# Layer 0 of a four-layer graph network: the degree sums in the text's order, the degrees ahead of a chunk's last products, and the second tile's rows ahead of the first pairs

## The chip, the core and the metric

The kernel runs on one core of one Trainium2 chip. The metric is the device time of one launch in microseconds, the median of several runs. The work is four layers in one program; the change touches the first of them alone.

## The reference, cut to what matters

`x` is 8 batches of 2048 nodes with 64 features, `adj` a 2048 x 2048 matrix, `H` a 2048 x 64 table of node to hyperedge. Layer 0 (the `h` that enters is a normalised, rectified `x`):

```python
def _L0_gnn_ref(x, H, adj, nhid, W, W_ind, a_node, a_gn, a_ge, fcW, fcb, av):
    h = x @ W
    s = leaky_relu(h @ a_node, 0.2)
    alpha = softmax(where(H.T[None] > 0, s[:, None, :], NEG), axis=-1)
    agg = einsum('ben,bnf->bef', alpha, h)
    beta = sigmoid((h @ a_gn)[:, None, :] + (agg @ a_ge)[:, :, None])
    all_he = elu(beta[..., None] * h[:, None] + (1 - beta[..., None]) * agg[:, :, None])
    deg = maximum(adj.sum(-1), 1.0)[:, None]
    industry = einsum('nm,bmf->bnf', adj / deg, x @ W_ind)
    ...                      # coefs1: softmax over the hyperedges of a node
    g = einsum('bne,benf->bnf', coefs1, all_he)
    pair = stack([industry, g], axis=2)
    ...                      # coefs2: softmax over the two, from tanh(pair @ fcW + fcb) @ av
    return einsum('bnk,bnkf->bnf', coefs2, pair)
```

Layers 1 to 3 follow: an attention over `adj`, three steps of message passing, and a polynomial graph convolution. They read the same `adj` and come after layer 0 in the data.

## The kernel before

Batches are taken two at a time, so a tile has 128 rows (2 x 64 features) and `NP` = 4 such pairs. Layer 0 goes through five stages, of which the change touches the second and the beginning of the third.

**First stage (to about 70 us).** The norm of `x` and the table `Y` = `x @ W_ind`, kept as two parts (`Y[0]`, `Y[1]`), together with the first quarter of the neighbour products.

**Second stage, the neighbour products (about 70 to 227 us).** `industry` is computed by column chunks of 512 nodes, `c` = 0 to 3. Chunk 0 belongs to the first stage. For chunks 1 to 3 the function `industry(c, own)` goes over 8 groups `g`. For each, `rows_of` requests a block `at` of 128 x 2 x 512 elements of `adjT` (512 KB) on GpSimd's DMA queue, into one of six buffers. A group has 16 products, 128x512 each, into four PSUM accumulators `acc`, one bank per batch pair, with no second buffer. A buffer `at` comes free when both the products and the degree sum of its group have read it. The degree of a node is the column sum of `adjT`: VectorE adds up the blocks in `ds` (L1066, 128x1024), and at the end of a chunk two products with a matrix of ones (L1078) sum over the partitions.

Between the products stand small pieces of other work, the `units`. Sixteen node tiles (`members`) each have two pieces `part` and one `end`. A `part` is: product `ph` (L1113), ScalarE copy `hi` (L1117), VectorE rest `lo` (L1118), the leaky relu `es` (L1121 to 1123) and VectorE product `hs` (L1124). The `end` is the product `pg` (L1136) and `pd` (L1140). `hi` and `lo` are stored to DRAM by SyncE, and have two buffers each. Other units build the lists of hyperedges (`ranks`, `numbers`, `widths`), the tables of hyperedge values (`table_1` to `table_5`) and the biases of the last layer (`biases`, which stores a tile `bs` of the tag `ev`).

At the end of a chunk `out_of` copies the accumulators into four tiles `ev` (tag `ev`, four buffers), takes the larger of degree and 1 (`rdeg`, L1080), and returns further units: the inverse by ScalarE's Ln and Exp (L1085, L1086), four products of `ev` and `rdeg` on VectorE (L1089), and four stores to `ind_dram` (L1090).

**Third stage, the pairs of node and hyperedge (about 227 to 360 us).** 18 tiles of 114 nodes, three groups of pairs each. `nodes(i)` makes the matrix `sT` that spreads a tile's nodes over its pairs: ScalarE's `tmp` (L823), then GpSimd's `sT` (L824); a tile `tmp` has one buffer. TensorE then makes `px`, VectorE `oT`, TensorE `pts` (against the identity `ident_r`) and `pm`, ScalarE the copy `S` and the sigmoid's tanh `be` (L1331). For each group of pairs TensorE makes `pd` and `pa`, VectorE `mix` and `ex`, ScalarE an exponential, GpSimd the weights, TensorE the sum `pgs`. These steps run in an order written out by hand.

**What sets the order.** The program is built by a layer that schedules instructions by their dependences and estimated readiness, engine by engine. An instruction that is issued through `InOrder` (the names `V`, `A`, `G`, `S` in layer 0) or passed to `keep_in_program_order` stays at its place in the text. Most units of the second stage, the degree sum and the evacuation among them, are issued through `nc.vector`, `nc.scalar` and the plain `mm`, and are placed by the scheduler.

The places in question, quoted short:

```python
if g > 0:
    nc.vector.tensor_tensor(ds, (was if g == 1 else ds).bitcast(FP), at.bitcast(FP), op=OP.add)
was = at
...
for step in (ranks, edges, turn, turned, shares, shared):
    step(0)
V, A = strict
next_nodes(1)
```

Of the kernel before, what the change touches and what calls it, by code (L numbers as in the profile page):

```python
# [16 lines left out]
P = 128  # L17
# [601 lines left out]
HN = N // 2  # L619
LN_EXP = "natural_log_exp_and_others"  # L620


# [148 lines left out]
def layer0(kit, hn, x1_dram, open_early, late_tile, between):  # L771
# [30 lines left out]
    etab = lst.tile([P, 2 * B], FR, name="etab")  # L802
    rden = lst.tile([P, LT, B], FP, name="rden")

    def of(i):
# [27 lines left out]
    with ExitStack() as sA:  # L833
# [107 lines left out]
        def rows_of(c, g):  # L941
            at = sp.tile([P, 2, CW], FR, tag="at", name="at")
            nc.gpsimd.dma_start(
                out=at,
                in_=t["adjT"][g * 2 * P : (g + 1) * 2 * P, cols(c)].bitcast(FR).rearrange("(k p) n -> p k n", p=P),
            )
            return at
# [91 lines left out]
        with ExitStack() as s1:  # L1039
# [7 lines left out]
            def industry(c, own):  # L1047

                for _ in range(2):
                    units.pop(0)()  # L1050
                acc, ds = accs(), dsp.tile([P, 2, CW], FR, tag="ds", name="ds")
                for g in range(NT // 2):
                    at = rows_of(c, g)
                    for k in range(2):
                        m = 2 * g + k
# [8 lines left out]

                    if g > 0:
                        nc.vector.tensor_tensor(ds, (was if g == 1 else ds).bitcast(FP), at.bitcast(FP), op=OP.add)  # L1066
                    was = at
                return out_of(c, acc, ds)

            def out_of(c, acc, ds):  # L1070
                ev = [sb.tile([P, CW], FP, tag="ev", name="ev", bufs=4) for p in range(NP)]
                for p in range(NP):
                    (nc.scalar.copy if p % 2 else nc.vector.tensor_copy)(ev[p], acc[p])
                deg = ds
                if c:
                    deg = ps.tile([P, CW], FP, tag="ph", name="deg", bufs=2)
                    for k in range(2):
                        mm(deg, ones_r, ds[:, k, :], start=k == 0, stop=k == 1)  # L1078
                rdeg = sb.tile([P, CW], FP, tag="rdeg", name="rdeg", bufs=1)
                nc.vector.tensor_scalar(rdeg, deg, 1.0, None, op0=OP.max)  # L1080
                nc.vector.tensor_reduce(bad[:, 3 + c : 4 + c], deg, AX.X, OP.min)
                nc.vector.tensor_scalar(bad[:, 3 + c : 4 + c], bad[:, 3 + c : 4 + c], 0.5, None, op0=OP.is_lt)

                def inverse():
                    nc.scalar.activation(rdeg, rdeg, AF.Ln, scale=2.0)  # L1085
                    nc.scalar.activation(rdeg, rdeg, AF.Exp, scale=-1.0)  # L1086

                def shares(p):
                    nc.vector.tensor_mul(ev[p], ev[p], rdeg)  # L1089
                    nc.sync.dma_start(out=ind_dram[p, :, cols(c)], in_=ev[p])  # L1090

                return [inverse] + [lambda p=p: shares(p) for p in range(NP)]

# [169 lines left out]
            units += [first_nodes, lambda: biases(3)]  # L1263
            own = out_of(0, acc, degs)
            for c in range(1, NCW):
# [9 lines left out]
    with ExitStack() as s0:  # L1275
# [8 lines left out]
        flat = lambda a: a.rearrange("p b f -> p (b f)")  # L1284
        ident_r = sb.tile([P, P], FR, name="ident_r", bufs=1)
        nc.vector.tensor_copy(ident_r, ident)
        def next_nodes(i):
# [100 lines left out]
        def done(i):  # L1388
            pt = tiles[i].pop("pb")
            for p in range(NP):  # L1390
                A.activation(gT[p][:, of(i)], pt[:, p, 0:LN], AF.Identity, bias=neg1)

        strict, V, A = (V, A), nc.vector, nc.scalar
        for step in (ranks, edges, turn, turned, shares, shared):
            step(0)
        V, A = strict
        next_nodes(1)

# [861 lines left out]
```

## Time and profile before

| | |
|---|---|
| median of 3 runs | 1966.83 us (1963.56 to 1970.12) |
| the profiled execution's own time | 1963.12 us |
| its span, first to last instruction | 1961.3 us |
| granted TensorE clock, mean | 0.989 |
| TensorE busy | 1900.6 us, 97% of the span |
| VectorE busy | 1190.7 us, 61% |
| ScalarE busy | 438.0 us, 22% |
| GpSimd busy | 315.4 us, 16% |

In the lines of the timeline each row has the start, the length, the engine, the line of the source, the operation, the tiles it writes and reads, the shape, the count, and in brackets the time for which the engine stood idle before it and what ended that. PE is TensorE, PEld its weight loads, DVE VectorE, ACT ScalarE, POOL GpSimd, SP SyncE; a q behind the name is the queue that issues. In rows by stage the clock is the share of the full TensorE clock that was granted. A matmul's listed length contains the part in which the next one already runs: of two 128x512 products in a row the second starts 0.23 us after the first.

### The profile page before, as it was taken

To read this page: it belongs to the slowest core of one execution; us is meant where nothing else is said; L and a number is where in the kernel's file an instruction comes from. 1 tells how busy PE (TensorE), PEld (TensorE's weight loads), DVE (VectorE), ACT (ScalarE), POOL (GpSimd) and SP (SyncE) were. 2 spreads that over 40 slices of the span, in tenths; PEclk is the share of its full clock that TensorE was granted. 3 is DMA by queue.
4 is the path that set the end of the run, shared out by engine and by line. 5 is a ranking of instruction groups with operands and counts; after the bars stand their busy time and mean duration, and the time that the engine had idled before them with its cause. 6 is when DMAs were issued, how large, how long until landed. Compare 5 with 4: busy or idle time off the path is not lost.

```text
span 1961.3 us, 23490 instructions
## 1 busy us (share of the span) xinstructions
PE 1900.6 (97%) x9060; PEld 1134.5 (58%) x9060; DVE 1190.7 (61%) x1917; ACT 438.0 (22%) x923; POOL 315.4 (16%) x435
## 2 busy tenths in 40 slices
PE   7999999889999999999999999999999999999997
PEld 6877777423323232257775477764577755677653
DVE  8676499768999998953326642346623275523365
ACT  6322355573111110111210111301112201112100
POOL 4111177310000000000002110012200022101122
PEclk9999899999999999999999999999999999999998
DMA  7556485473221212223101011100122011121000
GB/s 216 168 177 178 134 235 147 113 187 76 55 54 46 64 38 60 60 55 83 60 11 30 27 58 54 49 17 24 31 65 59 22 25 30 44 70 49 3 21 12
DMA packets 86362, 142.43 MB, mean 73 GB/s; under 512 B 33800, under 2 KB 34056, under 8 KB 83568
## 3 DMA queue, kind: packets, MB, share of 16 engines
q1 hardware_dynamic: 65200, 83.86, 14.3%
q0 software_dynamic: 21040, 56.98, 11.9%
q8 instruction: 73, 1.20, 0.3%
q14 instruction: 49, 0.40, 0.1%
HBM read 106.85 MB, written 37.09 MB: 73 GB/s over the span
## 4 chain that ended last, share of the span: by engine, by line
PE 66%; issue 17%; DVE 6%; DMA 4%; ACT 3%; POOL 3%; SPq 0%; POOLq 0%; DVEq 0%; ACTq 0%
PE acc L734 28%; PE u L734 14%; PE o L734 4%; PE py L734 3%; PE pd L734 2%; PE dn L734 2%; PE pgs L734 2%; PE acc L1058 2%; DMA at<-in_adjT 1%; PE var L734 1%; PE mean L734 1%; DMA den<-d_dram 1%; PE pv L734 1%; PE pf L734 1%; PE pm L734 1%
## 5 line engine op out<-in xcount | busy, mean ns | idle before, releaser
L734 PE MATMUL acc<-aT,parts 128*128 128x512 f32 x1664 | 448.2, 415 | 0.0
L734 PEld LDWEIGHTS acc<-aT,parts 128*128 128x128 f32 x1664 | 306.5, 188 | 102.2 <-issue 39.8
L2135 DVE TENSOR_TENSOR pr<-u,embf 128x512 f32<-128x512 f32 x256 | 170.7, 688 | 171.2 <-PE u L734 163.5
L734 PE MATMUL u<-W3f,y 64*128 64x512 f32 x1024 | 243.3, 589 | 0.0
L1733 DVE SCALAR_TENSOR_TENSOR pt<-R,wd,aT 128x1024 f32<-128x1024 f32 x192 | 236.2, 1280 | 9.5 <-DMA R<-r_dram 4.5
L734 PE MATMUL o<-pt,hS 128*64 128x512 f32 x1024 | 237.5, 599 | 0.8 <-DVE pt L1733 0.6
L734 PEld LDWEIGHTS u<-W3f,y 64*128 64x128 f32 x1024 | 101.8, 187 | 118.6 <-issue 118.6
L734 PEld LDWEIGHTS o<-pt,hS 128*64 128x64 f32 x1024 | 68.3, 136 | 160.2 <-issue 149.5
L734 PE MATMUL u<-W3f,v 64*128 64x512 f32 x512 | 137.9, 607 | 0.0
L2147 POOL TENSOR_TENSOR fold<-fold 128x256 f32<-128x256 f32 x64 | 47.7, 746 | 506.3 <-DVE fold L2146 506.3
L734 PE MATMUL dn<-pt,vd 128*32 128x512 f32 x1024 | 123.1, 598 | 0.0
L1952 DVE TENSOR_TENSOR yb<-py,cb_f 128x512 f32<-128x512 f32 x32 | 22.1, 691 | 161.4 <-PE py L734 161.4
L1058 PE MATMUL acc<-at,Y 128*128 128x512 f32 x384 | 105.1, 416 | 0.0
L734 PE MATMUL acc<-aTl,parts 128*128 128x512 f32 x384 | 96.5, 393 | 0.0
L2042 POOL TENSOR_TENSOR bq<-bq,xp 128x512 f32<-128x512 f32 x16 | 20.6, 1287 | 432.7 <-ACT xp L2025 432.7
L2139 DVE TENSOR_TENSOR pr<-pr 128x512 f32<-128x512 f32 x128 | 88.2, 689 | 2.2
L1733 DVE SCALAR_TENSOR_TENSOR pt<-R,wd,aTl 128x1024 f32<-128x1024 f32 x64 | 79.8, 1282 | 12.4 <-PE dn L734 8.2
L734 PEld LDWEIGHTS u<-W3f,v 64*128 64x128 f32 x512 | 51.4, 186 | 56.1 <-issue 34.1
L734 PEld LDWEIGHTS acc<-aTl,parts 128*128 128x128 f32 x384 | 72.1, 188 | 16.9
L1058 PEld LDWEIGHTS acc<-at,Y 128*128 128x128 f32 x384 | 70.6, 194 | 14.7 <-issue 1.3
L734 PEld LDWEIGHTS dn<-pt,vd 128*32 128x32 f32 x1024 | 26.9, 108 | 80.9 <-issue 77.1
L2113 ACT COPY y<-acc 128x512 f32<-128x512 f32 x16 | 9.4, 585 | 279.7 <-PE acc L734 279.7
(354 smaller groups left out, 2697.0 us busy)
## 6 DMA issues: line engine op xcount, KB each, us to landing
at<-in_adjT POOLq DMA_DIRECT2D x32, 512.0 KB, 5.5
raw<-in_adjT SPq DMA_DIRECT2D x64, 256.0 KB, 3.4
aT<-in_adjT POOLq DMA_DIRECT2D x12, 1024.0 KB, 5.5
xp<-xd SPq DMA_DIRECT2D x45, 256.0 KB, 3.0
R<-r_dram SPq DMA_DIRECT2D x14, 512.0 KB, 3.7
hlo<-lo_dram POOLq DMA_DIRECT2D x18, 235.1 KB, 3.9
hhi<-hi_dram POOLq DMA_DIRECT2D x18, 235.1 KB, 3.4
hi_dram<-hi SPq DMA_DIRECT2D x16, 264.0 KB, 3.4
```

The source lines that it names most:

```text
L734: one = self.nc.tensor.matmul(*args, **kw)
L1058: mm(acc[p], Y[h][:, m, p, :], at[:, k, :], start=m + h == 0, stop=m == NT - 1 and h == 1)
L1733: nc.vector.scalar_tensor_tensor(pt, R[b2], wd[:, m, b2 : b2 + 1], aT[m][:, s].bitcast(FP), op0=OP.max, op1=OP.mult)
L1952: nc.vector.tensor_tensor(yb, py, bias[:, None, :].to_broadcast([P, 4, P]), op=OP.add)
L2042: nc.gpsimd.tensor_add(bq, bq, xp)
L2113: nc.scalar.copy(y2, acc)
L2135: nc.vector.tensor_tensor(a, u[h], emb[:, i, 8 * w : 8 * w + 8, None].to_broadcast([P, 8, F]), op=OP.mult)
L2139: nc.vector.tensor_add(pr[h], pr[h], a)
L2147: nc.gpsimd.tensor_add(fold[:, :, 0:2, :], fold[:, :, 0:2, :], fold[:, :, 2:4, :])
```

## The change

The edits are these.

- The degree sum is issued through `V`, and ahead of its group's products instead of behind them.
- The two products for the degree are issued ahead of the last group's products and kept in the text's order; the maximum, Ln and Exp follow them there (`degrees`, `inverse`).
- In chunks 1 to 3 the accumulators of batch pairs 0 and 2 are multiplied by `rdeg` as VectorE reads them out of PSUM, and stored at once. Pairs 1 and 3 are copied by ScalarE as before and multiplied later, on GpSimd in chunk 3 and on VectorE otherwise. Chunk 0 keeps its copies and later products.
- The rounded identity `ident_r` is made at the start of layer 0, in a pool that lives to the end of the third stage.
- The table set that holds exp and tanh is loaded, and `next_nodes(1)` issued, ahead of tile 0's first steps in the third stage.

```diff
+TANH_EXP = "exp_and_others"
...
+    ident_r = lst.tile([P, P], FR, name="ident_r")
+    nc.vector.tensor_copy(ident_r, ident)
...
+                rdeg = None
                 for g in range(NT // 2):
                     at = rows_of(c, g)
+                    if g > 0:
+                        V.tensor_tensor(ds, (was if g == 1 else ds).bitcast(FP), at.bitcast(FP), op=OP.add)
+                    was = at
+                    if g == NT // 2 - 1:
+                        rdeg = degrees(c, ds)
                     for k in range(2):
...
-                    if g > 0:
-                        nc.vector.tensor_tensor(ds, (was if g == 1 else ds).bitcast(FP), at.bitcast(FP), op=OP.add)
-                    was = at
-                return out_of(c, acc, ds)
-
-            def out_of(c, acc, ds):
-                ev = [sb.tile([P, CW], FP, tag="ev", name="ev", bufs=4) for p in range(NP)]
-                for p in range(NP):
-                    (nc.scalar.copy if p % 2 else nc.vector.tensor_copy)(ev[p], acc[p])
-                deg = ds
-                if c:
-                    deg = ps.tile([P, CW], FP, tag="ph", name="deg", bufs=2)
-                    for k in range(2):
-                        mm(deg, ones_r, ds[:, k, :], start=k == 0, stop=k == 1)
+                return out_of(c, acc, rdeg)
+
+            def inverse(c, deg):
                 rdeg = sb.tile([P, CW], FP, tag="rdeg", name="rdeg", bufs=1)
                 nc.vector.tensor_scalar(rdeg, deg, 1.0, None, op0=OP.max)
+                nc.scalar.activation(rdeg, rdeg, AF.Ln, scale=2.0)
+                nc.scalar.activation(rdeg, rdeg, AF.Exp, scale=-1.0)
                 nc.vector.tensor_reduce(bad[:, 3 + c : 4 + c], deg, AX.X, OP.min)
                 nc.vector.tensor_scalar(bad[:, 3 + c : 4 + c], bad[:, 3 + c : 4 + c], 0.5, None, op0=OP.is_lt)
-
-                def inverse():
-                    nc.scalar.activation(rdeg, rdeg, AF.Ln, scale=2.0)
-                    nc.scalar.activation(rdeg, rdeg, AF.Exp, scale=-1.0)
+                return rdeg
+
+            def degrees(c, ds):
+                deg = ps.tile([P, CW], FP, tag="ph", name="deg", bufs=2)
+                for k in range(2):
+                    tc.keep_in_program_order(mm(deg, ones_r, ds[:, k, :], start=k == 0, stop=k == 1))
+                return inverse(c, deg)
+
+            def out_of(c, acc, rdeg):
+                ev = [sb.tile([P, CW], FP, tag="ev", name="ev", bufs=4) for p in range(NP)]
+                store = lambda p: nc.sync.dma_start(out=ind_dram[p, :, cols(c)], in_=ev[p])
+                late = {"rdeg": rdeg}
+                for p in range(NP):
+                    if p % 2:
+                        nc.scalar.copy(ev[p], acc[p])
+                    elif rdeg is None:
+                        nc.vector.tensor_copy(ev[p], acc[p])
+                    else:
+                        nc.vector.tensor_mul(ev[p], acc[p], rdeg)
+                        store(p)
 
                 def shares(p):
-                    nc.vector.tensor_mul(ev[p], ev[p], rdeg)
-                    nc.sync.dma_start(out=ind_dram[p, :, cols(c)], in_=ev[p])
-
-                return [inverse] + [lambda p=p: shares(p) for p in range(NP)]
+                    (nc.gpsimd if c == NCW - 1 else nc.vector).tensor_mul(ev[p], ev[p], late["rdeg"])
+                    store(p)
+
+                if rdeg is None:
+                    first = [lambda: late.update(rdeg=inverse(c, degs))]
+                    return first + [lambda p=p: shares(p) for p in range(NP)]
+                return [lambda p=p: shares(p) for p in (1, 3)]
...
-        ident_r = sb.tile([P, P], FR, name="ident_r", bufs=1)
-        nc.vector.tensor_copy(ident_r, ident)
...
+        tc.keep_in_program_order(nc.scalar.preload_act_table_set(TANH_EXP))
+        next_nodes(1)
         strict, V, A = (V, A), nc.vector, nc.scalar
         for step in (ranks, edges, turn, turned, shares, shared):
             step(0)
         V, A = strict
-        next_nodes(1)
```

More of the change, by code (lines that the diff above doesn't have):

```diff
@@ L1263, in layer0 @@
             units += [first_nodes, lambda: biases(3)]
-            own = out_of(0, acc, degs)
+            own = out_of(0, acc, None)
             for c in range(1, NCW):
```

## The prediction

> **What bounds the kernel now.** I read the page first, then busy time by stage, then the waits and the order of time inside layer 0, the only part that the change touches.
>
> ```profile
> span 1961.3 us, 23490 instructions
> PE 1900.6 (97%) x9060; PEld 1134.5 (58%) x9060; DVE 1190.7 (61%) x1917; ACT 438.0 (22%) x923; POOL 315.4 (16%) x435
> ```
>
> TensorE is occupied for 97% of the span, so a gain must come from its few idle microseconds or from stretches in which its clock is halved. By stage (columns: stretch, length, busy PE, PEld, DVE, ACT, POOL, granted clock, DMA):
>
> ```profile
> 69.00:117.00 48.00, 46.08 (x235) 36.19 (x234) 38.57 (x119) 12.50 (x46) 5.71 (x8) 1.00 0.65 196
> 117.00:172.00 55.00, 51.37 (x270) 40.81 (x269) 34.56 (x124) 13.60 (x48) 9.18 (x13) 1.00 0.63 185
> 172.00:227.00 55.00, 52.02 (x264) 41.25 (x263) 22.73 (x60) 13.73 (x32) 2.67 (x4) 0.94 0.31 94
> 227.00:246.00 19.00, 15.58 (x56) 12.81 (x55) 13.99 (x25) 9.37 (x19) 8.53 (x10) 0.65 0.99 304
> 246.00:360.00 114.00, 114.00 (x544) 81.01 (x543) 108.33 (x170) 62.78 (x164) 86.18 (x99) 1.00 0.58 165
> ```
>
> Chunks 1 to 3 of the neighbour products take the first three rows: TensorE idles 1.92 + 3.63 + 2.98 = 8.53 us. The fourth row is the start of the pairs: 3.42 us idle, and the clock at 0.65. From 246 on TensorE is full. The waits (who for whom: total, times, longest) say why it idles, the timeline shows the largest case:
>
> ```profile
> DVE ds L1066 <- DMA at<-in_adjT: 12.2, 8, 3.5
> PE ph L1113 <- DVE hs L1124: 7.6, 5, 2.9
> 126.63 0.71 POOL L943 DMA_DIRECT2D at<-in_adjT  x1 [7.40 <-PE acc L1058]
> 133.68 1.23 DVE L1066 TENSOR_TENSOR ds<-ds,at 128x1024 fp32r<-128x1024 f32 x1 [3.49 <-DMA at<-in_adjT]
> 134.82 0.42 DVE L1124 TENSOR_TENSOR hs<-ph,es 128x256 f32<-128x256 f32 x1
> 135.39 0.69 PE L1113 MATMUL ph<-W0x,hn 128*128 128x132 f32 x4 [2.92 <-DVE hs L1124]
> ```
>
> Counted by their loads, the degree sums run about five groups ahead of the products: this block is group 6 of chunk 2, whose products end near 172. VectorE stands 3.49 us before a block that has not landed, `hs` stands behind the sum, and TensorE waits 2.92 us for `hs`. At the start of the pairs:
>
> ```profile
> 228.94 0.52 PE L734 MATMUL pts<-ident_r,sT 114*128 114x114 f32 x3 [1.43 <-DVE bad L1082]
> 228.63 0.57 ACT L1073 COPY ev<-acc 128x512 f32<-128x512 f32 x1
> 230.09 1.28 ACT L1331 ACT_TABLE_LOAD   x1
> 231.55 0.61 ACT L823 ACTIVATE tmp<-slot,mid 114x384 f32<-114x384 f32 x1
> 232.26 1.23 POOL L824 TENSOR_SCALAR sT<-tmp,width 114x384 fp32r<-114x384 f32 x1 [43.00 <-ACT tmp L823]
> 233.55 0.69 PE L734 MATMUL px<-sT,Q 114*128 114x384 f32 x1 [1.99 <-POOL sT L824]
> 233.00:246.00 13.00, 12.45 (x37) 10.59 (x38) 8.76 (x14) 5.34 (x11) 7.80 (x10) 0.50 1.06 310
> ```
>
> The second tile's ranks wait for `sT`, that for `tmp`, that for the table load and the reciprocal before it. Then the pairs run 13 us at half clock.
>
> **What the Trainium skill says.** (1) "TensorE: Matmul & The Clock Gate", Part 1: the clock is full or half, granted by how busy a free-running window of 3.413 us was. The trace agrees: beside the row at 0.50, the clock is 0.57 in 181 to 185, after the 2.04 us gap that ends at 180.07. (2) The same page, "Architectural detail": ScalarE and VectorE take their queues strictly in order; the wait above shows it. (3) "ScalarE: Activation LUTs", "What ACT_TABLE_LOAD costs": 1283 ns for the load, and a drain for which I find no separate row; here it is 1.28 us and the next activation follows at 231.39.
>
> **The change, part by part.**
>
> *Sums in text order.* In the built order a chunk has 7 sums as before (21 x 1.22 us), now one before each group's products. A block is requested when the group six before it is done; 24 groups in 157 us are 6.6 us each and a landing takes about 5.5, so a block has landed some four groups (26 us) before its sum. VectorE no longer waits there. Of TensorE's six gaps (0.54, 1.38, 2.92, 0.70, 2.04, 0.95: together the 8.53) four lie behind such a sum: 1.38 + 2.92 + 2.04 + 0.95 = 7.29 us. The half-clock spell at 181 goes with its gap: 4 us x (1 - 0.57) = 1.7. Together **-9.0**. The sums move out of the full first chunk (11 run before 117, 7 do afterwards; VectorE is 38.6 of 48 us busy there) into the third, where it is busy 22.7 of 55. What is late next is the pipeline of members: the 2.27 us reduction of `MT` (L927), which began at 102.16, now stands before an `hs` and right behind the wait for a store (to 86.80). By the order of the queue that `hs` ends near 90.2 instead of 89.0; I charge **+1.0** (0 to 2).
>
> *Degrees ahead of the last products.* The two `deg` matmuls (0.46 us) stand four products before a chunk's end and can wait for sum 7. The last `hs` before that sum comes from a `ph` 3.7 us ahead of `deg`; `hi`, `lo`, `es`, `hs` and the sum take 3.4: about no wait. The banks `acc` are single, so the next chunk's first products now wait for the inverse: from the start of `deg`, 0.7 + maximum 0.7 + Ln 0.63 + `hi` 0.4 + Exp 0.63 + copy or product 0.69 = 3.8 us, while TensorE has 0.46 + 0.92 + ph 0.45 + pg 0.86 + ph 0.45 + pd 0.12 = 3.3 of other work: 0.5 at each of two turns, **+1.0** (0 to 4, as VectorE may be behind). Six PSUM copies (0.69) go from VectorE and two products of chunk 3 go to GpSimd (1.29 each by the nearest row, `bq` at L2042): off the path. The four stores stay, on SP; two move ahead of a member's stores, which nothing waits for within 5 us.
>
> *Identity early.* One cast (0.22 us) moves to the start, where VectorE idles 2.40 us before 7.92: nothing (0 to 0.2).
>
> *Start of the pairs.* Let T = 226.87 be the end of the products. `pts` no longer waits for the identity, but `pm` needs `oT`. `px` ends at T + 0.34, `oT` follows (0.55), `pm` takes 1.0, the first pair 0.9: TensorE stops at about T + 2.95. On ScalarE the queue is `ev` 3, table, `tmp`, `S`, `be`. In the built program `ev` 3 takes the buffer of the last bias store and must wait for its landing; before, that came at 227.92 and lay behind the reciprocal's Ln. Now the bias copy stands behind Ln and Exp, some 0.3 later: landing at T + 1.35. Then copy 0.57, table 1.28, `tmp` 0.61, `sT` 1.25 and 0.05 us between each: `px` of tile 1 at T + 5.2, against 233.55 = T + 6.7. GpSimd's two products end by T + 3.4, before `tmp` is there. So **-1.5**. The idle time is still about 2.2 us behind 1.0 us of 16-column products, so I keep the half-clock spell.
>
> Sum: -9.0 + 1.0 + 1.0 - 1.5 = **-8.5 us**. Nothing after the pairs is changed but the order of some loads on GpSimd, so it passes on whole. The sum is made against the profiled execution, which took 1963.12 us beside its span of 1961.3; the median of the runs is 1966.83, 3.7 above. On the median: 1966.8 - 8.5 = 1958.3, rounded to **1958**.
>
> **Rivals.**
> (a) *The clock stays full at the start of the pairs.* For: windows with gaps of 0.95 and 1.4 us (197, 228) did not halve it. Against: the idle of 2.2 us is as long as the 2.04 that did. Gain 13.65 / 2 = 6.8 more, four windows: 1951.5.
> (b) *The members' chain is the real bound.* Removing VectorE's wait only exposes the next one: `hi` and `lo` have two buffers, and VectorE also stood for their stores (to 86.80 and 96.73). For: VectorE is 80% busy in the first chunk. Against: it waited for blocks 12.2 us in all, and sums leave that chunk. Then 2 or 3 us are left of the gain: 1964.
> (c) *Slower: the turn of a chunk.* Products wait for the inverse, and that for sum 7 in a busy queue. It must eat the gain of 10.5 (9.0 + 1.5) and 5.9 more: 16.4 over three turns, 5.5 each, of which a half-clock window is 1.7; it decides from a wait of 3.8 us at every turn. The longest wait for VectorE's own work, without a block behind it, was 0.70. Then 1973.
> That the change doesn't do what it says is excluded by the built order for the sums.
>
> **How the numbers follow.** My case 58%, (a) 15%, (b) 20%, (c) 7%. Low end: (a) with both charges at zero, -17.3, gives 1949.5; high end: (b) with a scatter of 2 us, 1966. What a measurement of this kernel can tell from no change is 0.3%, 5.9 us. My case passes it nine times in ten, (a) always, (b) one time in four: faster 0.72, same 0.21, slower 0.07.
>
> **What would show it.** Right: in the waits, `ds <- DMA at` near zero; TensorE idle in the products under 4 us instead of 8.5; the pairs' first `px` of tile 1 about 5 us after the last product, behind a table load that waited for the bias store. Wrong: TensorE waiting for `ds` before `deg`, or for `ev` before a chunk's first products, by over 2 us; or `ph` waiting for `hs` as long as before.

## The result, and the profile after

The changed kernel took 1966.53 us (median of 12 runs, 1958.26 to 1972.23), the kernel before, beside it on the same chip, 1968.13 (12 runs, 1963.56 to 1973.2). The ratio of the two sets of runs is 0.9986, 95% interval 0.9970 to 1.0002 (the medians alone differ by 1.6 us): some 3 us were won, where 8.5 were forecast, and no change at all is not excluded. A later, longer comparison of the same two kernels (`r1_after`, 22 runs against 55) gives 0.9977, interval 0.9967 to 0.9987, or 4.5 us. The profiled execution of the changed kernel took 1963.18 us beside a span of 1961.3, as that of before did (1963.12 and 1961.3).

The page of the changed kernel, span and busy time of each engine:

```profile
span 1961.3 us, 23478 instructions
PE 1902.1 (97%) x9060; PEld 1132.4 (58%) x9060; DVE 1187.5 (61%) x1909; ACT 438.0 (22%) x923; POOL 318.6 (16%) x437
```

The same five stretches of layer 0 as in the prediction (stretch, length, busy PE, PEld, DVE, ACT, POOL, granted clock, DMA share, GB/s):

```profile
69.00:117.00 48.00, 46.16 (x234) 36.07 (x234) 34.75 (x115) 11.88 (x46) 5.71 (x8) 1.00 0.66 193
117.00:172.00 55.00, 52.45 (x265) 40.84 (x264) 33.32 (x119) 12.74 (x47) 9.33 (x13) 0.97 0.64 185
172.00:227.00 55.00, 53.77 (x285) 43.20 (x284) 29.09 (x68) 18.41 (x40) 5.75 (x7) 0.97 0.40 126
227.00:246.00 19.00, 17.35 (x64) 13.65 (x65) 14.23 (x23) 7.90 (x16) 12.67 (x15) 0.73 0.96 272
246.00:360.00 114.00, 112.77 (x533) 79.39 (x532) 109.10 (x172) 63.61 (x165) 84.81 (x97) 1.00 0.57 158
```

VectorE gave 4 us of work out of the first stretch and took 6 into the third, as said. TensorE is idle less in the second and third. But the clock of the second stretch, which was 1.00, is now 0.97, and 246 to 360, which was full, has 1.23 us of idle time: the pairs end 6 us earlier, so that the first gaps of their end lie inside it. The waits of the changed kernel (who for whom: total, times, longest; three lines of the list) show what came in place of `ds <- DMA at`, which is gone from the list:

```profile
DVE hi L1125 <- DMA hi_dram<-hi: 6.6, 4, 2.9
PE pf L735 <- DMA iv<-ind_dram: 5.3, 3, 2.6
PEld pm L735 <- DMA hlo<-lo_dram: 1.3, 1, 1.3
```

The first two were 1.9 and 2.7 us before; the third was not there. The timeline of TensorE, lines that waited:

```profile
86.97 0.69 PE L1132 MATMUL ph<-W0x,hn 128*128 128x132 f32 x4 [0.89 <-DVE es L1141]
111.88 0.72 PE L1132 MATMUL ph<-W0x,hn 128*128 128x132 f32 x4 [0.65 <-DVE rank L897]
116.75 0.70 PE L1088 MATMUL deg<-ds,ones_r 128*128 128x512 f32 x2 [0.30 <-DVE ds L632]
120.49 2.36 PE L1067 MATMUL acc<-at,Y 128*128 128x512 f32 x9 [0.24 <-ACT ev L1097]
158.37 0.72 PE L1132 MATMUL ph<-W0x,hn 128*128 128x132 f32 x4 [2.13 <-DVE rank L916]
...
227.78 0.69 PE L735 MATMUL px<-sT,Q 114*128 114x384 f32 x1 [1.63 <-POOL sT L827]
241.02 0.28 PE L735 MATMUL pm<-hlo,sT 114*128 114x16 f32 x1 [0.87 <-DMA hlo<-lo_dram]
```

With one more of 0.13 us (`deg` at 170.31) the gaps in the products come to 4.3 us, where they were 8.5. Of these, 3.7 us lie ahead of a `ph` and 0.7 at the two turns of a chunk, that is, between the last products of one chunk and the first of the next (`deg` and the first `acc`). The longest, 2.13 us ahead of `ph`, is put down to `rank`. VectorE's own timeline tells what `rank` stood behind:

```profile
156.31 0.07 DVE L1125 MEMSET hi<- 128x8 f32 x1 [2.66 <-DMA hi_dram<-hi]
157.77 0.54 DVE L916 TENSOR_TENSOR rank<-rank,pm 114x384 f32<-114x384 f32 x1 [1.40 <-issue]
157.79 0.07 DVE L1125 MEMSET lo<- 128x8 f32 x1
```

A memset of 65 ns waits 2.66 us for the store of an earlier member (issued 151.19, landed 5.06 us later), and everything else on VectorE stands behind it. For the 1.40 us ahead of `rank` the profile names no cause, but they end with the other memset: the store of `lo` landed at 157.73, and its memset starts 0.06 us later, just as that of `hi` starts 0.06 us after its own store (156.25). So VectorE stood about 4 us for two stores, TensorE waits for `rank`, and a half-clock spell of 3.4 us follows at 159.2. This is the wait on which the rest of this document turns.

**By stage.** Worked out from the traces. A chunk runs from its first product to the next chunk's first (the third: to its last product), "start" from the last product to the ranks of the sixth tile of pairs, "output" from the ranks of the last tile to layer 1's first attention product. In brackets: idle TensorE, and half of TensorE's occupied time at half clock, which is what the halved clock cost.

| us | before | before again | after | after again |
|---|---|---|---|---|
| chunk 1 | 50.0 (1.9, 0) | 50.3 (2.2, 0) | 51.0 (2.1, 0) | 50.4 (1.5, 0) |
| chunk 2 | 54.1 (3.6, 0) | 55.3 (3.1, 1.7) | 54.9 (2.3, 1.7) | 54.2 (3.2, 0) |
| chunk 3 | 52.4 (3.0, 3.4) | 55.7 (3.0, 6.8) | 47.4 (0, 1.7) | 53.8 (0, 8.5) |
| start | 37.0 (3.4, 6.3) | 35.8 (3.4, 4.8) | 34.8 (2.9, 5.0) | 35.9 (3.8, 5.1) |
| output | 105.3 (19.7, 4.3) | 105.9 (19.8, 4.8) | 110.2 (21.6, 7.3) | 107.4 (19.9, 6.2) |

Idle times of one kernel repeat within 1 us (1.7 in the output stage), the loss to the clock does not: chunk 3 of one and the same kernel lost 1.7 us in one execution and 8.5 in another.

### The profile page after: what moved, and what is told of

Same layout as the page of the kernel before. It is cut to its first block, busy times and chain, and to the rows that moved or that the text cites. A ratio compares the mean times of both kernels' runs of the same rounds, so it can differ in the third digit from the quotient of the medians.

```text
span 1961.3 us, 23478 instructions
## 1 busy us (share of the span) xinstructions
PE 1902.1 (97%) x9060; PEld 1132.4 (58%) x9060; DVE 1187.5 (61%) x1909; ACT 438.0 (22%) x923; POOL 318.6 (16%) x437
## 4 chain that ended last, share of the span: by engine, by line
PE 68%; issue 16%; DVE 5%; DMA 5%; ACT 4%; POOL 2%; SPq 0%; POOLq 0%; DVEq 0%; ACTq 0%
PE acc L735 28%; PE u L735 14%; PE acc L1067 4%; PE o L735 4%; PE py L735 3%; PE pgs L735 2%; PE dn L735 2%; PE pd L735 2%; PE var L735 1%; PE mean L735 1%; DMA den<-d_dram 1%; DMA iv<-ind_dram 1%; PE pv L735 1%; DMA W3f<-in_L_gnn_weight 1%; PE pm L735 1%
```

## The experiments

Each kernel goes by a label (`r1_sums`). All ratios are to the kernel before, run beside it on the same chip; its medians there were 1966.5 to 1971.2 us.

### Both kernels once more

> The kernel before, unchanged, for a second profile. Theory 1 (the waits belong to the kernel): TensorE idles 8 to 9 us in the neighbour products again, the last product starts at 226.5 +- 1, the last tile of pairs reaches its ranks at 351.4 +- 2, the output stage follows with a half-clock spell near 379 only. Theory 2 (the places are a matter of how the 3.4 us clock windows happen to fall): idle times of waits are as before, but the half-clock spells lie elsewhere, and milestones differ from the first profile by 3 us or more. Time by both: ratio 1.000 within 0.003.

Measured: 0.9990 (0.9976 to 1.0004), 14 runs; the last product started at 231.14 instead of 226.49, since chunks 2 and 3 had 17.1 us at half clock instead of 6.8 (5.1 us more lost to the clock).

> The changed kernel, unchanged, for a second profile. Theory 1: the last product starts near 222.7, the last tile of pairs near 345.1, 6 us ahead of before; then 3 us go in half-clock windows at the end of the pairs and 2.6 us in a wait for the fifth load of the industry term, so that the output stage ends only 1.3 us ahead, as in the first profile. Theory 2: the 6 us are there again, but one or both of the later losses are absent or lie elsewhere, because a window decides them. Time: ratio 0.9986 within 0.003.

Measured: 0.9977 (0.9967 to 0.9987). The table above has both. The waits of the products and of the start are there again, those of the output stage too; but the 6 us lead at the end of the pairs is 0.3 here against the first profile of before (4.1 against the second), eaten by half-clock spells at 203.6 and 213.9. Theory 2 holds for the clock, theory 1 for the waits. A single profile of this kernel can't be read to better than about 5 us unless idle time and clock are kept apart.

### The sums alone, and sums with the new start

```diff
                     at = rows_of(c, g)
+                    if g > 0:
+                        V.tensor_tensor(ds, (was if g == 1 else ds).bitcast(FP), at.bitcast(FP), op=OP.add)
+                    was = at
...
-                    if g > 0:
-                        nc.vector.tensor_tensor(ds, (was if g == 1 else ds).bitcast(FP), at.bitcast(FP), op=OP.add)
-                    was = at
```

> The kernel before with one part of the change: the degree sums in the text's order, ahead of each group's products; degrees, evictions and the start of the pairs stay as before. Theory of the prediction: no wait of the sums for a block, TensorE idles under 3 us in the products, the last product starts 8 to 9 us earlier than before, near 218; time 8 us less (ratio 0.9960). Rival (the members' chain, with its stores to memory, is the real bound): the wait of VectorE for those stores takes over, the last product starts 3 to 4 us earlier, near 222.7 as in the changed kernel; time 3 us less (0.9985).

Measured: 1961.4 us, 0.9964 (0.9953 to 0.9976): 7 us. The stretches of this kernel (the third ends with its products):

```profile
69.00:117.00 48.00, 47.04 (x241) 37.33 (x240) 36.11 (x116) 12.89 (x47) 5.70 (x8) 1.00 0.64 192
117.00:172.00 55.00, 54.34 (x284) 42.92 (x283) 37.41 (x134) 15.49 (x54) 10.60 (x15) 1.00 0.67 197
172.00:222.50 50.50, 50.50 (x244) 41.00 (x244) 23.62 (x52) 11.17 (x26) 1.42 (x2) 0.86 0.28 91
```

TensorE idles 0.96 + 0.66 + 0.00 us instead of 8.5. The rival is out for this part: its ratio, 0.9985, lies outside the interval, and chunk 2 alone is 3 us shorter than before. The last product came at 222.48, where the rival had it, and not at 218; but that is chunk 3, which ran at a clock of 0.86 and lost 6.8 us to it.

The second kernel adds the identity, the early table load and the early `next_nodes(1)` to that.

> The changed kernel with the degrees, the inverse and the evictions back where they were (sums in order and the start of the pairs as changed). Theory of the prediction: moving the degrees costs 1 us, so this is 1 us faster than the changed kernel (ratio 0.9980 to 0.9985 beside 0.9986), and the chunk ends at 117.8 and 171.9 come back instead of 118.0 and 173.1. Rival: the fused evictions free VectorE and are what gains in the third chunk; without them the last product starts 2 us or more later than in the changed kernel (over 224.7).

Measured: 1959.63 us, 0.9962 (0.9948 to 0.9975). The chunks end at 117.4 and 169.8, and the last product starts at 221.25, so the rival is out. The start did not get shorter (36.9 us; ranks of tile 1 at 6.6 us after the last product, before 6.7): with the inverse still behind the products, the table load and `tmp` stand behind it. The sum of both parts lies 3 us below the changed kernel, and its products idle 2.4 us instead of 4.3 and 4.7. So the third part, the early degrees, costs some 3 us net by the ratios, whose intervals overlap, and 2 us by the idle time, where I had charged 1.0. Of the 2.4 us, 1.4 lie ahead of a `ph` that waits for `rank`, as in the changed kernel: that wait comes without early degrees too.

### What do the early degrees cost? Three attempts that missed

Three buffers for the members' tiles, the room taken from the degree sums:

```diff
-                    hi = sb.tile([P, BF_ + 2 * B], FR, tag="hi", name="hi")
-                    lo = sb.tile([P, BF_ + 2 * B], FR, tag="lo", name="lo")
+                    hi = sb.tile([P, BF_ + 2 * B], FR, tag="hi", name="hi", bufs=3)
+                    lo = sb.tile([P, BF_ + 2 * B], FR, tag="lo", name="lo", bufs=3)
...
-        dsp = sA.enter_context(tc.tile_pool(name="degrees", bufs=2, reuse_waits="tile"))
+        dsp = sA.enter_context(tc.tile_pool(name="degrees", bufs=1, reuse_waits="tile"))
```

> The changed kernel with three buffers instead of two for each of the members' tiles hi and lo (their room comes from the degree sums, which get one buffer instead of two). Theory S (VectorE's wait for the members' stores stands ahead of sum 7 and of the ranks, and is what the early degrees cost): the wait of hi for its store, 6.6 and 3.9 us in the two profiles, goes to under 1 us; TensorE idles 2 us or less in the products instead of 4.3 and 4.7, the degree products wait under 0.3 us; the time falls to that of the sums alone, ratio 0.9960 to 0.9970. Rival U (the turn of a chunk itself costs: the degree products for sum 7, the next products for the inverse): the waits before degrees and first products stay, 1 us or less is won, ratio 0.9975 to 0.9985.

Measured: 0.9978 (0.9965 to 0.9991), idle 3.8 us, `deg` waited 1.65 us. That is rival U's number, but it does not decide, because the edit did not take the wait away: `hi` still waited 4.0 us for its store. With a third buffer free, the built order has the memset of a member one member earlier, where the store that it needs had again not landed: it ran at 163.97, the store had landed at 163.91. The same edit on the sums alone:

> The kernel before with the sums in the text's order and the same buffers (three for hi and lo, one for the sums), degrees and start of the pairs as before. Theory S: the sums alone leave 2.0 us of VectorE's wait for the stores and 1.5 us of idle TensorE, so at most 1 us is to be won: ratio 0.9955 to 0.9965, beside 0.9964 without the buffers. Rival U: the same. If it gains as much as the same buffers do in the changed kernel, the stores cost both alike and are not what the early degrees cost.

Measured: 0.9970 (0.9955 to 0.9986), beside 0.9964: nothing.

The last sum of a chunk one group earlier in the changed kernel:

```diff
+                    if g == NT // 2 - 2:
+                        nxt = rows_of(c, g + 1)
+                        V.tensor_tensor(ds, ds.bitcast(FP), nxt.bitcast(FP), op=OP.add)
```

> The changed kernel with the last degree sum of each chunk one group (3.7 us of products and more) earlier in VectorE's order, ahead of the products of group 6 instead of group 7; the degree products stay. Theory T (the degrees cost because they must wait for the last sum, which stands behind the members' work in VectorE's queue): the wait of the degree products, 0.3 us at the first turn and 0.1 to 2.7 at the second, is gone, and with it the half-clock spell at 171 that followed it in two of five profiles; TensorE idles 3 us or less in the products, ratio 0.9960 to 0.9970. Rival V (VectorE is simply late, by its waits for the members' stores): the same idle time comes back as waits of the members' products for VectorE, ratio 0.998.

Measured: 0.9985 (0.9973 to 0.9996), idle 5.0 us. The timeline of this kernel around the second turn of a chunk:

```profile
160.56 2.47 DVE L632 TENSOR_TENSOR ds<-ds,at 128x1024 fp32r<-128x1024 f32 x2
...
162.95 0.42 DVE L1141 SCALAR_TENSOR_TENSOR lo<-ph,hi 128x256 fp32r<-128x256 f32 x1
...
164.49 0.07 DVE L1129 MEMSET hi<- 128x8 f32 x1 [1.12 <-DMA hi_dram<-hi]
165.17 0.15 DVE L1141 SCALAR_TENSOR_TENSOR lo<-ph,hi 128x4 fp32r<-128x4 f32 x1 [0.62 <-issue]
...
166.49 0.71 PE L1092 MATMUL deg<-ds,ones_r 128*128 128x512 f32 x2 [2.15 <-DVE es L1144]
```

Both last sums are done at 163.03, and `deg` still starts at 166.49, behind `es`. By the code `deg` takes one of the two PSUM buffers named `ph`, and so it waits for a member's `lo`, `es` and `hs` to have read theirs; these stand behind the memset that waits for the store. Theory T is out, V fits.

The evictions as copies again, with the early degrees kept:

```diff
-                    elif rdeg is None:
+                    else:
                         nc.vector.tensor_copy(ev[p], acc[p])
-                    else:
-                        nc.vector.tensor_mul(ev[p], acc[p], rdeg)
-                        store(p)
...
-                return [lambda p=p: shares(p) for p in (1, 3)]
+                return [lambda p=p: shares(p) for p in range(NP)]
```

> The changed kernel with early degrees, but all four evictions as copies again, which need no inverse, and the four products with the inverse afterwards, as before. Theory T: the next chunk's first products no longer wait (0.2 us), little else: idle time 4 us or more, ratio 0.9975 to 0.9985. Rival W (the evictions bound to the inverse are what costs): idle time falls to the 1.5 to 2.4 us of the kernels without early degrees, ratio 0.9960 to 0.9970.

Measured: 0.9975 (0.9962 to 0.9988), idle 3.7 us, `deg` waited 1.99 us. Rival W is out: to bind the evictions to the inverse costs about what the trace says, 0.24 us at a turn.

### The memsets taken away

```diff
-                    hi = sb.tile([P, BF_ + 2 * B], FR, tag="hi", name="hi")
-                    lo = sb.tile([P, BF_ + 2 * B], FR, tag="lo", name="lo")
+                    hi, lo = parts[i % 3]
...
-                    for v in (hi, lo):
-                        nc.vector.memset(v[:, BF_ + B :].bitcast(FP), 0.0)
                     part(0)
...
+            parts = [[sb.tile([P, BF_ + 2 * B], FR, name=f"{n}{k}", bufs=1) for n in ("hi", "lo")] for k in range(3)]
+            for v in parts[0] + parts[1] + parts[2]:
+                nc.vector.memset(v[:, BF_ + B :].bitcast(FP), 0.0)
```

(and one buffer for the degree sums, as above).

> The changed kernel without the members' memsets: three lasting pairs of hi and lo tiles, whose zero columns are written once ahead of the first member (room as in the run with three buffers). Theory S2 (the wait of VectorE for a member's store, which the scheduler puts ahead of the last sum and of the readers of ph, is what the early degrees cost): VectorE has no wait for a store, the degree products at the second turn wait under 0.5 us instead of 1.4 to 2.7, TensorE idles 2 us or less in the products, ratio 0.9955 to 0.9970. Rival X (VectorE has too much work at the turn, about 4 us per turn for maximum, reduction, evictions): idle time stays at 4 us, ratio 0.9975 to 0.9985.

Measured: 1957.2 us, 0.9941 (0.9920 to 0.9961; 6 runs), clear of the changed kernel's 0.9967 to 0.9987. The stretches, cut at the ends of the chunks:

```profile
69.50:118.00 48.50, 48.31 (x250) 38.42 (x248) 32.39 (x103) 14.28 (x51) 6.42 (x9) 1.00 0.65 192
118.00:168.30 50.30, 50.30 (x264) 39.98 (x264) 34.17 (x108) 13.58 (x49) 9.90 (x14) 1.00 0.69 199
168.30:216.00 47.70, 47.70 (x250) 38.50 (x250) 25.24 (x58) 12.87 (x29) 1.56 (x3) 0.96 0.33 107
216.00:254.00 38.00, 31.55 (x137) 23.91 (x136) 26.56 (x42) 16.19 (x36) 25.25 (x29) 0.87 0.93 266
```

The products idle 0.19 us in all, at one turn of a chunk, and VectorE has no wait for a store. It does the same work as before at each turn and delays TensorE nowhere: rival X is out, and S2 is shown for the idle time.

> The kernel before with the sums in the text's order and the same lasting tiles without memsets. Theory S2: without early degrees nothing of the products stands behind VectorE's wait, so at most 0.5 us is won: ratio 0.9960 to 0.9967. If it wins 2 us or more, the store waits cost both orders alike.

Measured: 1954.8 us, 0.9935 (0.9913 to 0.9957), idle 0. Here my expectation missed: 5.7 us below the sums alone, where 0.5 were expected. The profiles, one of each, differ by 1.5 us of idle time (1.5 to 0) and 5.1 in what chunk 3 loses to the clock (6.8 to 1.7 us); whether the latter is chance, one profile of each can't tell. By the sign set ahead, more than 2 us here means that the waits for stores cost both orders. By the ratios they do, 7 us with early degrees (0.9977 to 0.9941) and 5.7 without; by idle time it is 4.2 to 4.5 and 1.5. That they are what sets the early degrees apart is shown by the idle time alone. With the stores out of the way both orders can be compared cleanly: the three chunks take 146.2 us with early degrees and 145.1 without, at the same loss to the clock (1.7). Of the 1.1 us, 0.5 are only the third chunk's `deg`, which late degrees have behind the last product; so the early degrees themselves cost about 0.6 us in the products.

### Where the start of the pairs loses what it gains

`r4_zeros` reached its last product 12 us ahead of `r1_after` (4.6 by idle time, 6.8 by the clock of chunk 3) and then took 38.6 us for the start, longer than any kernel above. TensorE's timeline there, lines that waited:

```profile
216.90 0.28 PE L735 MATMUL pm<-hhi,sT 114*128 114x16 f32 x1 [0.38 <-DVE oT L1320]
220.75 0.61 PE L735 MATMUL px<-sT,Q 114*128 114x384 f32 x1 [1.66 <-POOL sT L827]
234.56 0.38 PE L735 MATMUL pm<-hlo,sT 114*128 114x16 f32 x1 [4.41 <-DMA hlo<-lo_dram]
```

The 0.87 us of the changed kernel have become 4.41. The rows `hlo` of the third tile are issued at 225.03 and land 9.5 us later. On SP's queue in that time:

```profile
217.52 0.55 SPq L632 DMA_DIRECT2D xd<-in_xT  x1
...
219.19 1.14 SPq L632 DMA_DIRECT2D xd<-in_xT  x2
```

These are the three 1 MB fills of `x1`; they land at 224.6, 229.5 and 232.6. The next kernel issues them later, on GpSimd's queue:

```diff
-        for p in range(1, NP):
-            S.dma_start(out=x1_dram[p], in_=t["xT"][p])
...
+            if k == 1 and i in (4, 6, 8):
+                G.dma_start(out=x1_dram[i // 2 - 1], in_=t["xT"][i // 2 - 1])
```

> The changed kernel without memsets, and the three 1 MB fills of x1 on GpSimd's queue during tiles 4, 6 and 8 of the pairs instead of on SP's at their start. Theory F (the fills stand before the rows on the DMA engines): the wait for hlo, 4.4 us, falls below 1 us, TensorE idles 3 us or less at the start of the pairs instead of 6.45; 2 to 4 us less than without the move (0.9941), ratio 0.992 to 0.993. Rival G (the rows are late because their issue waits on GpSimd's queue for a buffer): the wait stays above 3 us, ratio 0.994.

Measured: 1954.2 us, 0.9905 (0.9885 to 0.9925). The start takes 34.0 us and idles 2.0; its stretch:

```profile
218.30:252.00 33.70, 31.67 (x138) 24.25 (x136) 26.08 (x41) 15.97 (x34) 25.47 (x29) 0.85 0.69 212
```

No tile waits for its rows: theory F is shown by the wait, though the intervals of the two times still touch (0.9920 to 0.9961 against 0.9885 to 0.9925). The times differ by 3.0 us, as expected; that the ratio fell further than expected is due to the kernel before, which took 1971.2 us beside this run and 1968.7 beside `r4_zeros`.

### The clock in chunk 3

```diff
-                for i in range(LT):
-                    mm(pn[0:LN, i, :], MT[:, of(i)], kept["ea"][0:E, B : 2 * B], start=True, stop=True)
+                thin.extend([... one or two such products each ...] + [ends])
...
                                 mm(acc[p], Y[h][:, m, p, :], at[:, k, :], start=m + h == 0, stop=m == NT - 1 and h == 1)
+                            if thin:
+                                thin.pop(0)()
```

(`ps_e` in the same way; each step of the table ahead of its bias instead of behind it.)

> The changed kernel with the narrow products of the third chunk (16 passes of 1 column, 36 of 8 columns) spread among its neighbour products, one or two between two pairs of them, instead of two blocks of 2 and 4 us. Theory C (a 3.4 us window filled with narrow products halves the clock as an idle one does, and which windows are hit is chance): no half-clock spell between 198 and 224, where the six profiles had 3.4 to 17 us of them (mean 9.7, worth 4.8 us); time 2 to 5 us less than the changed kernel, ratio 0.9955 to 0.9970, and the runs lie closer together. Rival: the halved clock there has another cause (the idle time ahead of it); spells stay, ratio 0.998.

Measured: 1962.9 us, 0.9972 (0.9959 to 0.9984), 14 runs from 1959.5 to 1965.6. Ahead of the halved clocks of `r1_after` its TensorE was doing this (timeline):

```profile
202.39 2.47 PE L1215 MATMUL ps_e<-avf,the 128*128 128x1 f32 x16
204.72 6.57 PE L1067 MATMUL acc<-at,Y 128*128 128x512 f32 x16
...
212.30 5.70 PE L1225 MATMUL pn<-ea,MT 64*114 64x8 f32 x36
217.93 5.49 PE L1067 MATMUL acc<-at,Y 128*128 128x512 f32 x12
```

and its stretches show TensorE fully occupied throughout (PE busy is the length of each) with the clock at 0.54 and 0.50 behind the narrow blocks:

```profile
200.00:204.00 4.00, 4.00 (x27) 3.36 (x26) 0.00 (x0) 1.87 (x4) 0.00 (x0) 0.95 0.05 8
204.00:211.00 7.00, 7.00 (x21) 5.56 (x20) 1.40 (x2) 0.76 (x3) 0.00 (x0) 0.54 0.11 42
211.00:214.00 3.00, 3.00 (x27) 2.66 (x25) 0.00 (x0) 0.58 (x1) 0.00 (x0) 0.98 0.04 15
214.00:224.00 10.00, 10.00 (x35) 8.70 (x36) 2.44 (x3) 0.00 (x0) 0.00 (x0) 0.50 0.07 23
```

With the narrow products spread, the same part of chunk 3:

```profile
195.00:204.00 9.00, 9.00 (x48) 6.86 (x47) 4.84 (x6) 2.64 (x6) 0.00 (x0) 1.00 0.08 31
204.00:214.00 10.00, 10.00 (x56) 7.92 (x56) 1.40 (x2) 2.26 (x4) 0.00 (x0) 1.00 0.16 59
214.00:220.00 6.00, 6.00 (x32) 3.92 (x30) 1.44 (x3) 1.85 (x3) 0.00 (x0) 1.00 0.01 3
```

Up to 220 theory C holds: there is no spell in the two places where `r1_after` has them. But the spread did not keep the clock to the end of the chunk: a half-clock spell of 13.7 us begins at 220.5, inside the stretch for which none was expected, after a window in which TensorE was busy throughout with wide products, six of 8 columns and eight of 128. It costs the chunk 2.2 us, against 1.7 and 8.5 in the two profiles of the changed kernel. So blocks of narrow products go with the halved clock here, and how many wide ones between them would do is open. In time the gain over the changed kernel is not resolved: the ratio lies inside that kernel's interval.

### Behind the pairs

```diff
+            if last < j < last + 3:
+                fill = ps.tile([P, B, F], FP, tag="pa", name="fill", bufs=2)
+                for n in range((0, 3, 7)[j - last]):
+                    mm(flat(fill), tiles[LT - 1]["oT"][:, 0:P], flat(tab), start=True, stop=True)
...
-            nc.sync.dma_start(out=iv, in_=ind_dram[p, :, cols(c)])
+            (nc.gpsimd if 1 < i < 7 else nc.sync).dma_start(out=iv, in_=ind_dram[p, :, cols(c)])
...
-            if i in (1, 4, 8):
-                p = 1 + i // 4
+            for p in range(1, NP) if i == 5 else ():
                 nc.gpsimd.dma_start(out=x1_dram[p], in_=gT[p], accum_op=OP.add)
```

> The changed kernel with two edits behind the pairs: ten products whose result nothing reads, in the two gaps at the end of the pairs (0.85 and 1.79 us), and five loads of the industry term issued on GpSimd's queue ahead of the three 1 MB sums into x1. Theory D (the first profile's losses after the pairs belong to the kernel): the half-clock spell at 360 and the wait of 2.6 us for the fifth load are gone, time 3 to 5 us less than the changed kernel, ratio 0.9955 to 0.9965. Theory C: the spell there came in three profiles of six by chance, so the edits are worth 1 to 2 us, ratio 0.997 to 0.998.

Measured: 0.9967 (0.9953 to 0.9981), beside 0.9977 for the changed kernel. The value lies between the two theories, and the interval reaches into both. The losses that the edits aim at, in the first profile of the changed kernel:

```profile
358.50 1.11 PE L735 MATMUL pgs<-mix,S 128*114 128x512 f32 x2 [0.85 <-POOL mix L632]
361.41 2.05 PE L735 MATMUL pgs<-mix,S 128*114 128x512 f32 x2 [1.79 <-POOL mix L632]
...
376.35 1.13 PE L735 MATMUL pf<-iv,fcWf 64*128 64x512 f32 x4 [2.53 <-DMA iv<-ind_dram]
...
389.66 1.13 PE L735 MATMUL pf<-iv,fcWf 64*128 64x512 f32 x4 [2.60 <-DMA iv<-ind_dram]
```

The `pgs` at 361.41 takes 2.05 us instead of 1.11, at half clock; the kernel before had the same two gaps (0.85 and 1.79 us) and kept its clock. The idle time of the output stage falls from 19.9 and 21.6 us to 15.7, the stage from 107.4 and 110.2 to 102.7.

> The kernel before with the two edits behind the pairs alone. Theory D (the output stage takes back what the change wins, so before has nothing to lose there): no gain, ratio 0.999 to 1.001. Theory C (the stage has its waits in every kernel): 2 to 4 us less, ratio 0.9980 to 0.9990, and its idle time falls from 19.7 us to about 16, as in the changed kernel with the same edits.

Measured: 0.9981 (0.9972 to 0.9990), idle time of the stage 16.4 us: the waits were there in the kernel before too, and theory D is out as it was put, that before has nothing to lose there. About 1 us of it remains (see the point "It passes on whole" below).

> The kernel before with the sums in the text's order and the two edits behind the pairs (ten products in the gaps at their end, five loads of the industry term ahead of the sums into x1). If the parts add: 7 us from the sums and 2 to 4 from the edits, ratio 0.9940 to 0.9955, faster than the changed kernel by 5 us. If what is won ahead of the output stage is lost in it (theory D), the edits bring more here than the 2 us that they brought to the changed kernel; if clock windows fall by chance, the same.

Measured: 1957.4 us, 0.9951 (0.9936 to 0.9965; 6 runs). That agrees with parts that add, 0.9945 (0.9964 times 0.9981).

### Versions that beat both

> The changed kernel without the memsets and with the two edits behind the pairs. If S2 holds and the parts add: ratio 0.9935 to 0.9955, level with or ahead of sums plus edits (0.9951), since the early degrees then keep their 2 us at the start of the pairs. If X holds: 0.9960 to 0.9970, as the changed kernel with the two edits (0.9967).

Measured: 1953.2 us, 0.9929 (0.9908 to 0.9950).

> Sums in the text's order, no memsets, the two edits behind the pairs; no early degrees. By S2 and by X alike 0.9940 to 0.9955, as sums plus edits without the lasting tiles (0.9951).

Measured: 1952.6 us, 0.9915 (0.9894 to 0.9935). Both of these are faster than the ranges expected.

> The same with the two edits behind the pairs. Theory F and parts that add: ratio 0.990 to 0.992, the fastest of all, ahead of sums, no memsets and edits (0.9915). Rival G: 0.993, as without the move (0.9929).

Measured: 1951.1 us, 0.9884 (0.9865 to 0.9903; 6 runs, 1947.9 to 1952.0), 20 us ahead of the kernel before beside it (1971.2). It is the changed kernel with lasting zero columns, the fills of `x1` moved and the two edits behind the pairs. Whether it is ahead of the version with late degrees (1952.6 us, 0.9915) is not settled: the times differ by 1.5 us, each beside another run of the kernel before. Nor does it speak for early degrees, because late degrees with the fills moved were not tried. In the four pairs of kernels that differ in the early degrees (in three of them in the new start of the pairs too), the early ones are slower each time, by 1.2 to 3.1 us, though the intervals overlap: 0.9977 against 0.9962 (`r1_after`, `r1_sums_pairs`), 0.9967 against 0.9951 with the two edits, 0.9941 against 0.9935 without memsets, 0.9929 against 0.9915 with both.

## Why the prediction was wrong, point by point

- **Sums in text order, -7.3 us of gaps: right.** Idle time in the products went from 8.5 to 1.5 us in the kernel that has this part alone, its time down by 7.
- **The half-clock spell at 181, -1.7: wrong.** The spell went, another came at 159, and chunks 1 to 3 lost 3.4 us to the clock in the first profile of either kernel and 8.5 in the second. So the two kernels lost the same, and nothing was won. I took one profile's spell for a property of the kernel. The Trainium skill's page "TensorE: Matmul & The Clock Gate", Part 1, says that the window runs free and that one kernel therefore differs from run to run; the prediction cited the page and did not draw this from it. The clock deserved a width in the range, not a term in the sum.
- **The turn of a chunk and the members, +1.0 each: the step that failed, "about no wait".** By these charges 3.2 us of idle time were to remain in the products; 4.3 and 4.7 did. I had counted the work between the last `ph` and sum 7 (3.4 us) and one late `ph`, but not what VectorE waits for besides: the stores of the members, behind the memsets. At the two turns TensorE idles 0.7 and 2.0 us in the two profiles of the changed kernel, and 2.3 and 3.3 in `r2_narrow` and `r2_fill_iv`, which have the same turns. In the second profile VectorE stood 1.6 and 0.5 us for stores (up to the memsets at 164.54 and 165.22), and `deg` waited 1.42 us at 169.08. In the first profile the missing time is not at the turns but ahead of `ph`: 3.7 us, of which 2.13 in one wait behind `rank` (2.6 and 1.6 in the second). This was rival (b)'s wait, in part at rival (c)'s place. I had seen it (VectorE stood "for their stores", to 96.73), and gave it to the first chunk alone, though the trace of before has it twice just ahead of the second turn:

```profile
158.92 0.07 DVE L1106 MEMSET lo<- 128x8 f32 x1 [0.98 <-DMA lo_dram<-lo]
166.14 0.07 DVE L1106 MEMSET hi<- 128x8 f32 x1 [0.95 <-DMA hi_dram<-hi]
```

Without the memsets the products idle 0.19 us in all: the arithmetic was sound where its assumption holds.

- **The one `ph` of the first chunk: right in size.** It waited 0.96 us at 87.85 in the kernel with the sums alone, 0.89 at 86.97 in the changed one.
- **Start of the pairs, -1.5: right at the place, lost behind it.** The ranks of tile 1 came 4.7 us after the end of the last product in both profiles (forecast 5.2; before, 6.7 in both); the bias store landed 0.65 us after it and not 1.35. But the third tile then waited 0.87 and 1.76 us for its rows. I had passed GpSimd's and ScalarE's queues there and not the DMA engines, which the row that I showed gave at 0.99 to 1.06 busy. That the clock would be halved there: right in both profiles (10.2 us in either).
- **"It passes on whole": wrong.** In the first profiles of the two kernels the lead was 6.2 us at the end of the pairs, 1.3 behind the output stage and none at the end of the span (1961.3 us in both); in the second ones 4.1, 2.6 and 3.3. With no edits behind the pairs the stage took 105.8 to 110.2 us in eight profiles with early degrees (mean 108.2) and 105.3 to 107.0 in six with late ones (106.1). Of these 2.1 us, 1.0 are lost to the clock (means 6.0 against 4.9) and 1.1 are idle time of TensorE (20.9 against 19.8), which goes with its waits for the loads of the industry term (`pf` for `iv`: 4.5 against 3.2). With the edits, which move these loads, the order is reversed (means 103.6 and 105.8, three each). The clock part may be the fall of the windows; why the loads come later with early degrees stays open.
- **The rivals.** (a) did not happen. (b) named the right wait; its number, 1964, is closest, and its gain of 2 or 3 us is what was measured. (c) named one of the places, but its price, 5.5 us a turn, was far off.

In one line: some 1.5 us more idle time in the products behind the members' stores, 1.7 for the spell, about 2 between the pairs and layer 1: of 8.5 us some 3 are left. Of these three the first is shown by taking the memsets away; the other two are read from profiles.

## What to carry to other kernels

Before an instruction is moved ahead on an in-order engine, look up what its producer's engine *waits* for in that time, not only what it works on: a 65 ns memset that waits for a buffer's store can hold a whole chain, and a further buffer does not help if the scheduler uses it to place the memset earlier. Where a stretch gets shorter, its transfers must fit into the shorter time as well; here a DMA share near 1.0 in the row of the stretch announced the next wait. Where the clock is granted by windows, keep idle time and clock apart and take at least two profiles before a spell is counted.

## What the runs showed of the hardware that I had not expected

- A stretch in which TensorE never idles can still lose its clock: behind blocks of 1-column and 8-column products the clock was 0.54 and 0.50 for 6.8 and 10.2 us (`r1_after`), and every profile that had these blocks whole has such a spell (3.4 to 17 us between 196 and 225). With the same products spread between wide ones it stayed at 1.00 up to 220.5, and then fell all the same (`r2_narrow`).
- One and the same kernel lost 1.7 us to the clock in one chunk of one execution and 8.5 in another. The 34 runs of the changed kernel lie between 1958 and 1972 us, the 14 with the narrow products spread between 1959.5 and 1965.6.
- Loads of 235 KB took 9.0 and 9.5 us to land while three 1 MB fills ran, where the page's medians are 3.3 and 3.6 (`r4_zeros`); with the fills moved the same loads took 4.7 and 4.1 (`r5_zeros_x1late`).
